# Retention layer and quantised FFN on one core: order of block 0's last products and turns, a weight-rounding clump moved by a step, the last FFN's first products, and the tail's rstd on ScalarE

## The chip, the cores and the metric

The kernel runs on 1 core of one Trainium2 chip. The metric is the device time of one execution in microseconds (us). Times given as "the median" come from 3 runs; everything read from the trace comes from one profiled execution.

## The reference, cut to what matters

The input `x` has 4 sequences of 1024 tokens with 512 features, so 4096 rows. All arithmetic is in float32.

```python
def layernorm(x): return (x - mean(x)) / sqrt(var(x) + 1e-5)          # over the 512 features

def retention(x):
    q, v = x @ Wq.T, x @ Wv.T
    ret = scan(v)              # per sequence: state = lam * state + v_t, one lam for each head
    y = layernorm(q * ret) * gamma + beta
    return (y * silu(x @ Wg.T)) @ Wo.T

def ffn(x):                    # gate_w, up_w, down_w are first rounded to float8 e4m3 values
    gate = silu((x @ gate_w) * gate_scale)
    return ((gate * ((x @ up_w) * up_scale)) @ down_w) * down_scale   # 512 -> 1536 -> 512

x1  = x  + layernorm(retention(layernorm(x)))
out = x1 + layernorm(ffn(layernorm(x1)))
```

## The kernel before, in words

The 4096 rows are cut into 8 blocks of 512 tokens (`NB = 8`, `TB = 512`), each of four subtiles of 128 tokens (`NS = 4`). The 512 features are four chunks of 128 (`NC = 4`), and the FFN's 1536 hidden features are 12 chunks (`NI = 12`). Blocks are software-pipelined. In the main loop over `t` the FFN of block t (`f`, class `Ffn`) runs with the retention part of block t+1 (`b`, class `Retention`), the first steps of block t+2 (`n`) and the last steps of the FFN of block t-1 (`l`). The inner loop over `i` from 0 to 11 takes one hidden chunk in each step: `f.gate(i)` (tile `pfg`), one product of the retention of `b`, `f.up(i)` (tile `pfu`), and `f.down(i - f.lag)` (tiles `pd`; lag 2, in the last block 4).

The order on every engine is the order of the Python code: all instructions are kept in program order by the wrapper `InOrder`. So an instruction that waits holds up all that stand behind it on its engine. Each helper call puts its instructions at that place in the queue of each engine that it uses.

Steps that the change touches:

- `turn_x(s)` turns a subtile of the next block's normalised x on TensorE (tile `ptx`). `keep_x(s)` copies it into `xnT`, on ScalarE for s = 0 and 1 and on VectorE for s = 2 and 3. The pool that holds `xnT` has one buffer for it, so block 1's `xnT` takes the place of block 0's, whose last reader is the product `a.gate(3)` (tile `pg`).
- `var()` is the matmul that averages the squares (`sqsum`, summed on GpSimd) over the features; ScalarE takes the square root and `rstd_y()` is VectorE's reciprocal of 128x512.
- `q(c)` is the product with `wq_sb` (tile `pq`); `y_of(c)` is its VectorE product with the scanned `ret`.
- `turn_x1n(s)` (tile `pt`), `upper_of(s)` (ScalarE) and `rest_of(s)` (VectorE) make the two parts of `x1nT`, which `f.gate` and `f.up` read. Two parts, a rounded one and its remainder, stand in for one float32 operand; all products of the FFN run over both.
- `rounds(3)` rounds one of the 18 weight pieces to float8 values: three VectorE operations on 128x1024 (tile `scr`). `units()` issues the two ScalarE operations of 128x1024 that belong to it; `rounds(3)` calls it straight away unless `now=False`. All but the first eight pieces are loaded by SP's queue when an earlier piece is finished.
- `halves()` splits a sum in two parts (`half`): a copy on ScalarE, then a subtraction on VectorE. In step i = 4 the two parts feed the two matmuls of `var()`.
- In the tail, after the loop, each subtile s goes through `scale`, `stats` (VectorE), `rstd`, `norm` and `add`. `rstd(s)` is `rstd_in_place`: two operations on a 128x1 operand on GpSimd. `norm` runs on ScalarE for s < 3 (`shift_scale`: three operations) and on VectorE for s = 3.

Of the kernel before, what the change touches and what calls it, by code (L numbers as in the profile page):

```python
# [14 lines left out]
AF = mybir.ActivationFunctionType  # L15
# [8 lines left out]
def retention_ffn_sandwich(  # L24
# [23 lines left out]
    NI = I // P  # L48
    TB = 512
    NS = TB // P  # L50
# [15 lines left out]
    class InOrder:  # L66
# [9 lines left out]
    pe, dve, act, pool, sp = (  # L76
        InOrder(e) for e in (nc.tensor, nc.vector, nc.scalar, nc.gpsimd, nc.sync)
    )
# [16 lines left out]
    def load_square(src, name):  # L95
        w = wpool.tile([P, NC, D], F32, tag=name, name=name)
        v = src.rearrange("(c p) f -> p c f", p=P)
        for h in range(2):
            sp.dma_start(w[:, 2 * h : 2 * h + 2, :], v[:, 2 * h : 2 * h + 2, :])
        return w  # L100
# [3 lines left out]
    wq_sb = load_square(wqT, "wq_sb")  # L104
# [29 lines left out]
    eps_sb = const.tile([P, 1], F32, tag="eps_sb", name="eps_sb")  # L134
# [80 lines left out]
    def units():  # L215

        while open_units:
            _, c = open_units.pop(0)
            act.activation(c, c, AF.Relu, bias=neg_low)
            act.activation(c, c, AF.Identity, scale=1.5 * 2.0**20, bias=low_unit)  # L220

    def rounds(n, now=True):
        for _ in range(n):
            next(rounding, None)
            if now:
                units()
# [35 lines left out]
    def rstd_in_place(var, n):  # L262
        pool.tensor_scalar(var, var, EPS, 1.0, ALU.add, ALU.mult)
        pool.tensor_tensor(var, var, nhalf[:, :n], ALU.pow)
# [17 lines left out]
    def project(po, w, col, parts, tokens=slice(None)):  # L282


        out = po.rearrange("p (g j) -> p g j", j=Q) if len(parts[0].shape) == 4 else po
        for c in range(NC):
            for h, part in enumerate(parts):
                pe.matmul(
                    out[:, tokens], w[:, c, ts(col, P)], part[:, c, tokens],
                    start=(c == 0 and h == 0), stop=(c == NC - 1 and h == len(parts) - 1),  # L290
                )
# [3 lines left out]
    def ps_tile(name, home="pa"):  # L295
        return homes[home].tile([P, TB], F32, tag=home, name=name)
# [20 lines left out]
    class Retention:  # L317
# [88 lines left out]
            )  # L406
            dve.tensor_copy(carry[:, c : c + 1], ret[:, TB - 1 : TB])

        def q(self, c, home="pa"):
            self.pq[c] = ps_tile(f"pq_{self.t}_{c}", home)  # L410
            project(self.pq[c], wq_sb, c, [self.by_chunk])

        def y_of(self, c):

# [133 lines left out]
    class Ffn:  # L548
# [68 lines left out]
        def rstd(self, s=None):  # L617
            if s is None:
                rstd_in_place(self.mv[:, :, 1], NS)
            else:  # L620
                rstd_in_place(self.mv[:, s, 1:2], 1)

        def norm(self, s, center=center_scale):
            center(self.d[s], self.d[s], self.mv[:, s, :])

# [46 lines left out]
    early, later = slice(0, TB // Q // 2), slice(TB // Q // 2, TB // Q)  # L672
# [17 lines left out]
    b = Retention(1)  # L690
# [33 lines left out]
        b.norm_x(s, True)  # L724
    rounds(6, now=False)
    a.gate(2, "pf")
    a.var()
    a.rstd_y()
    a.silu(2)
    b.new_xnT()  # L730
    b.turn_x(0, "pd0")
    b.turn_x(1, "pd1")
    a.gate(3, "pf")
    b.turn_x(2, "pd2")
    b.turn_x(3, "pd3")
    b.keep_x(0)
    b.keep_x(1)
    b.keep_x(2, dve.tensor_copy)
# [39 lines left out]
    b.q(0, "pf")  # L778
    a.turn_x1n(1)
    a.upper_of(1)  # L780
    a.turn_x1n(2)
    a.upper_of(2)
    a.x1_moments(3)
    a.x1n_of(3)
    a.rest_of(1)
    b.y_of(0)
    a.rest_of(2)
    b.q(1, "pf")
    rounds(3, now=False)
    a.turn_x1n(3)  # L790
    a.upper_of(3)
    units()
    a.rest_of(3)
    b.y_of(1)
# [4 lines left out]
    l = None  # L799
    for t in range(NB):  # L800
        f, n = Ffn(a), None
        for i in range(NI):
            if t > 0 and (t > 1 or i):
                (f if i else l).rest((i - 1) % NI)
            if t == 0 and i == 0:
                n = Retention(2)
# [32 lines left out]
                next(search)  # L839

            if b and t == 0 and i < 2:
                b.q(i + 2)
                b.y_of(i + 2)
            if b and t > 0 and i < 3:
                b.v(i + 1)
# [15 lines left out]
                    n.shift()  # L861
            if b and i == 4:
                b.halves()
                b.g_of(1)
                b.var()
            if b and i == 5:
# [27 lines left out]
                b.turn_x1n(3, "pf")  # L894
                b.upper_of(3)
            if t == 0:
                if i < 8:
                    rounds(3, now=i == 3)
                f.rest(i)
                if i < 3:  # L900
                    n.stats(i)
# [36 lines left out]
                n.send_x(2 * i - 9)  # L938
            if n and i == (9 if t else 7):
                n.fetch_x()  # L940
            if b and not n and i == 11:
                b.turn_x1n(3)
                b.upper_of(3)
            if b and i == 11:
                b.rest_of(3)
            if n and i == 11:
                n.q(0)
# [3 lines left out]
                f.sums()  # L951
            if f.lag <= i < (NI if b else NI - 1):
                f.down(i - f.lag)
            elif l and i < 2:
                l.down(NI - 2 + i)
            if b and i == 4 and 0 < t < NB - 2:
                n = Retention(t + 2)
            if t == 2 and i == 1:
# [5 lines left out]
        l, a, b = f, b, n  # L964
# [14 lines left out]
    for s in range(NS):  # L979
        l.scale(s)  # L980
        l.stats(s)
        l.rstd(s)
        if s < NS - 1:
            l.norm(s, shift_scale)
        if s == 2:
            l.add(0, dve)
    l.add(1, dve)
    l.add(2, dve)
    l.norm(3)
    l.add(3, dve)  # L990

# [43 lines left out]
```

## Time and profile before

| what | value |
|---|---|
| median of 3 runs | 1011.26 us (1011.08 to 1011.37) |
| the profiled execution's own time | 1010.72 us |
| its span, first to last instruction | 1008.9 us |
| TensorE (PE) busy | 991.4 us, 98% of the span |
| VectorE (DVE) busy | 633.8 us, 63% |
| ScalarE (ACT) busy | 328.0 us, 33% |
| GpSimd (POOL) busy | 241.2 us, 24% |
| mean granted TensorE clock | 0.997 |
| DMA | 73.79 MB, 73 GB/s over the span |

All instructions carry line L74, that of the wrapper, so instructions are told apart by their tiles. A product of four 128x512 float32 matmuls shows in the trace as 8 matmuls, 3.43 us long where TensorE has no gap (`pq`, `pg`, `pv`, `po`). A product of the FFN, 8 matmuls of 128x512 over the two parts, takes 1.81 to 1.83 us (`pfg`, `pfu`, `pd`). A turn of four 128x128 takes 0.44 us. Times of single instructions below are from the span's start.

### The profile page before, as it was taken

Reading aid. Unit: us, or ns where it says so; the run is one execution under the profiler, and the core shown is the slowest. Engines: PE = TensorE matmul, PEld = TensorE weight load, DVE = VectorE, ACT = ScalarE, POOL = GpSimd, SP = SyncE. Lnnn points to the kernel's source line nnn. Section 1 sums busy time; section 2 is a strip of 40 time slices with the busy share of each in tenths; the row PEclk is TensorE's granted clock in tenths of the full one; section 3 lists DMA queues with packets and bytes.
Section 4 is the critical chain, followed back from the end, with each engine's and each line's share of the span. In section 5 each row is a group of like instructions: output and inputs, shape, how many; then the busy total and the mean of one; then the engine's idle time right before and its main releaser. Section 6 shows DMA issues by size and latency. Waiting matters only on the chain.

```text
span 1008.9 us, 9809 instructions
## 1 busy us (share of the span) xinstructions
PE 991.4 (98%) x3502; PEld 652.7 (65%) x3502; DVE 633.8 (63%) x945; ACT 328.0 (33%) x489; POOL 241.2 (24%) x290
## 2 busy tenths in 40 slices
PE   9999989999999999999999999999999999999997
PEld 7454756666666666666666666666666756766885
DVE  5996878436767286663767547674576735746444
ACT  3546555524765124111321113211141111412222
POOL 1405131202322042221403114131142302213021
PEclk9999999999999999999999999999999999999999
DMA  9312213400126004250113402043020520004021
GB/s 302 106 62 97 97 58 89 141 1 21 63 74 157 0 22 146 84 146 1 39 56 104 115 1 84 11 128 92 0 84 32 136 63 7 37 22 125 1 84 42
DMA packets 62608, 73.79 MB, mean 73 GB/s; under 512 B 5856, under 2 KB 36320, under 8 KB 62560
## 3 DMA queue, kind: packets, MB, share of 16 engines
q1 hardware_dynamic: 60976, 72.24, 23.6%
q10 hardware_dynamic: 1584, 0.94, 0.4%
q8 instruction: 27, 0.44, 0.2%
q14 instruction: 21, 0.17, 0.1%
HBM read 43.53 MB, written 29.62 MB: 73 GB/s over the span
## 4 chain that ended last, share of the span: by engine, by line
PE 91%; DVE 3%; POOL 2%; ACT 2%; DMA 1%; issue 0%; ACTq 0%; SPq 0%; POOLq 0%; DVEq 0%
PE pfu L74 17%; PE pfg L74 16%; PE pd L74 16%; PE pv L74 11%; PE pq L74 10%; PE pg L74 10%; PE po L74 10%; DVE scr L74 1%; POOL sqsum L74 1%; DMA xnT<-mx 1%; POOL x L74 1%; POOL mv L74 0%; DVE st L74 0%; PE var L74 0%; ACT scr L74 0%
## 5 line engine op out<-in xcount | busy, mean ns | idle before, releaser
L74 PE MATMUL pfu<-x1nT,up_sb 128*128 128x512 f32 x768 | 217.1, 425 | 0.0
L74 PE MATMUL pfg<-x1nT,gate_sb 128*128 128x512 f32 x768 | 190.2, 390 | 1.1 <-ACT x1nT L74 0.7
L74 PE MATMUL pd<-down_sb,fuse 128*128 128x512 f32 x720 | 188.4, 403 | 0.0
L74 PEld LDWEIGHTS pfu<-x1nT,up_sb 128*128 128x128 f32 x768 | 145.4, 189 | 56.0 <-issue 29.2
L74 PEld LDWEIGHTS pfg<-x1nT,gate_sb 128*128 128x128 f32 x768 | 143.9, 188 | 31.7 <-DVE x1nT L74 1.0
L74 PEld LDWEIGHTS pd<-down_sb,fuse 128*128 128x128 f32 x720 | 135.4, 188 | 38.2 <-issue 10.8
L74 ACT CAST fuse<-gate 128x512 fp32r<-128x512 f32 x90 | 55.7, 619 | 275.0 <-DVE gate L74 275.0
L74 ACT ACTIVATE gate<-pfg,gs_sb 128x512 f32<-128x512 f32 x96 | 65.9, 687 | 225.1 <-PE pfg L74 225.0
L74 DVE SCALAR_TENSOR_TENSOR gate<-pfu,us_sb,gate 128x512 f32<-128x512 f32 x96 | 71.7, 747 | 105.9 <-PE pfu L74 105.7
L74 PE MATMUL pv<-xnT,wv_sb 128*128 128x512 f32 (+1 forms) x280 | 114.9, 556 | 1.3 <-ACT xnT L74 1.1
L74 PE MATMUL pq<-xnT,wq_sb 128*128 128x512 f32 x256 | 114.9, 592 | 0.0
L74 PE MATMUL pg<-xnT,wg_sb 128*128 128x512 f32 x256 | 114.8, 592 | 0.0
L74 PE MATMUL po<-wo_sb,y 128*128 128x512 f32 x256 | 114.5, 592 | 0.0
L74 POOL TENSOR_SCALAR mv<-mv 128x1 f32<-128x1 f32 (+1 forms) x77 | 19.0, 247 | 315.4 <-DVE mv L74 314.7
L74 PEld LDWEIGHTS pv<-xnT,wv_sb 128*128 128x128 f32 x280 | 52.7, 189 | 48.6 <-issue 44.0
L74 DVE TENSOR_TENSOR fuse<-gate,fuse 128x512 fp32r<-128x512 f32 x90 | 79.4, 883 | 6.9 <-ACT fuse L74 6.9
L74 PEld LDWEIGHTS po<-wo_sb,y 128*128 128x128 f32 x256 | 48.4, 189 | 50.1 <-issue 47.4
L74 PEld LDWEIGHTS pg<-xnT,wg_sb 128*128 128x128 f32 x256 | 48.4, 189 | 49.6 <-issue 47.0
L74 PEld LDWEIGHTS pq<-xnT,wq_sb 128*128 128x128 f32 x256 | 47.9, 189 | 49.0 <-issue 47.4
L74 POOL TENSOR_TENSOR x<-x,x1n 128x512 f32<-128x512 f32 x32 | 49.2, 1536 | 44.3 <-DVE x1n L74 35.4
L74 DVE TENSOR_TENSOR_SCAN ret<-lam,pv 128x512 f32<-128x512 f32 x16 | 19.5, 1220 | 54.5 <-PE pv L74 54.5
L74 DVE BATCH_NORM_STATS2 st<-x 128x6 f32<-128x512 f32 x64 | 43.5, 680 | 13.6 <-POOL x L74 11.3
(112 smaller groups left out, 923.0 us busy)
## 6 DMA issues: line engine op xcount, KB each, us to landing
kept<-x SPq DMA_DIRECT2D x32, 256.0 KB, 2.1
x<-kept SPq DMA_DIRECT2D x32, 256.0 KB, 3.9
x<-in_x SPq DMA_DIRECT2D x28, 256.0 KB, 3.8
out<-d SPq DMA_DIRECT2D x27, 256.0 KB, 2.0
xnT<-mx SPq DMA_DIRECT2D x24, 256.0 KB, 4.7
mxs<-xs SPq DMA_DIRECT2D x84, 64.0 KB, 1.8
x1n<-mxs SPq DMA_DIRECT2D x21, 256.0 KB, 2.6
mx<-xn SPq DMA_DIRECT2D x20, 256.0 KB, 2.1
```

What stands on the lines that cost most here:

```text
L74: return lambda *args, **kwargs: tc.keep_in_program_order(op(*args, **kwargs))
```

## The change

There are five edits.

1. In block 0, the four `turn_x` of block 1 stand ahead of `a.var()`; before, two stood behind it and two behind `a.gate(3)`.
2. `b.q(1)` is cut into two halves of 256 tokens, set between the turns of `x1n`; the first half of `b.q(2)` moves from the main loop to the place behind the last turn, in the memory of `pd0`.
3. In the main loop of t = 0, the rounding of one piece moves from the end of step 3, with its ScalarE part at once, to step 4 behind `b.halves()`, with its ScalarE part issued later in that step by `units()`.
4. In t = 6, the last step's turn of `x1n` moves behind `f.down(9)`, and `f.down(10)` follows it there; it stood in the first step of t = 7, and `l.down(11)` moves from the second step of t = 7 to the first.
5. In the tail, `rstd(s)` becomes a square root on ScalarE and a 128x1 reciprocal on VectorE, and the additions of s = 0, 1 and 2 all stand behind the loop.

```diff
-        def q(self, c, home="pa"):
-            self.pq[c] = ps_tile(f"pq_{self.t}_{c}", home)
-            project(self.pq[c], wq_sb, c, [self.by_chunk])
+        def q(self, c, home="pa", tokens=slice(None)):
+            if c not in self.pq:
+                self.pq[c] = ps_tile(f"pq_{self.t}_{c}", home)
+            project(self.pq[c], wq_sb, c, [self.by_chunk], tokens)
...
+        def rstd_by_root(self, s):
+            var = self.mv[:, s, 1:2]
+            act.activation(var, var, AF.Sqrt, bias=eps_sb)
+            dve.reciprocal(var, var)
...
     a.gate(2, "pf")
+    b.new_xnT()
+    for s in range(NS):
+        b.turn_x(s, f"pd{s}")
     a.var()
     a.rstd_y()
     a.silu(2)
-    b.new_xnT()
-    b.turn_x(0, "pd0")
-    b.turn_x(1, "pd1")
     a.gate(3, "pf")
-    b.turn_x(2, "pd2")
-    b.turn_x(3, "pd3")
     b.keep_x(0)
...
     a.turn_x1n(1)
     a.upper_of(1)
+    b.q(1, "pf", early)
     a.turn_x1n(2)
     a.upper_of(2)
+    b.q(1, "pf", later)
     a.x1_moments(3)
     a.x1n_of(3)
     a.rest_of(1)
     b.y_of(0)
     a.rest_of(2)
-    b.q(1, "pf")
     rounds(3, now=False)
     a.turn_x1n(3)
     a.upper_of(3)
+    b.q(2, "pd0", early)
     units()
     a.rest_of(3)
     b.y_of(1)
...
             if b and t == 0 and i < 2:
-                b.q(i + 2)
+                b.q(i + 2, tokens=slice(None) if i else later)
                 b.y_of(i + 2)
...
             if b and i == 4:
                 b.halves()
+                if t == 0:
+                    rounds(3, now=False)
                 b.g_of(1)
                 b.var()
...
             if t == 0:
-                if i < 8:
-                    rounds(3, now=i == 3)
+                if i < 8 and i != 3:
+                    rounds(3, now=False)
                 f.rest(i)
...
-            if b and not n and i == 11:
-                b.turn_x1n(3)
-                b.upper_of(3)
-            if b and i == 11:
+            if b and n and i == 11:
                 b.rest_of(3)
...
             if f.lag <= i < (NI if b else NI - 1):
                 f.down(i - f.lag)
-            elif l and i < 2:
-                l.down(NI - 2 + i)
+            elif l and i < 2 and (b or i == 0):
+                l.down(NI - 2 + i if b else NI - 1)
+            if b and not n and i == 11:
+                b.turn_x1n(3)
+                b.upper_of(3)
+                b.rest_of(3)
+                f.down(NI - 2)
...
     for s in range(NS):
         l.scale(s)
         l.stats(s)
-        l.rstd(s)
+        l.rstd_by_root(s)
         if s < NS - 1:
             l.norm(s, shift_scale)
-        if s == 2:
-            l.add(0, dve)
-    l.add(1, dve)
-    l.add(2, dve)
+    for s in range(NS - 1):
+        l.add(s, dve)
     l.norm(3)
     l.add(3, dve)
```

## The prediction

> **What bounds the kernel now.** The page first: TensorE is busy nearly throughout, so a gain lies in its gaps or in the tail behind its last matmul.
>
> ```profile
> PE 991.4 (98%) x3502; PEld 652.7 (65%) x3502; DVE 633.8 (63%) x945; ACT 328.0 (33%) x489; POOL 241.2 (24%) x290
> ```
>
> Then TensorE's waits (total us, times, longest). Apart from the start and waits of 0.3 or less there are six, and the edits stand at all of them: block 0's `var` (0.9), the turns (`pt`) and first FFN product after block 0 (1.0, 0.7, 0.5), `var` of step 4 (3.6), the last turn at 930 us (0.8).
>
> ```profile
> PE var L74 <- ACT half L74: 3.6, 1, 3.6
> ...
> PE pt L74 <- ACT x1n L74: 1.0, 1, 1.0
> PE var L74 <- POOL sqsum L74: 0.9, 1, 0.9
> PE pt L74 <- DVE x1n L74: 0.8, 1, 0.8
> PE pfg L74 <- ACT x1nT L74: 0.7, 1, 0.7
> PE pfg L74 <- DVE x1nT L74: 0.5, 1, 0.5
> ```
>
> Third, the timeline (start, us, instruction) at the longest: ScalarE, then TensorE. `half` sits behind two `scr`, and the `pfu` after the gap takes 3.57 us where 1.98 is usual (1.81 without the overlap of neighbours). The windows table says why: clock 0.50.
>
> ```profile
> 130.87 1.14 ACT L74 ACTIVATE scr<-scr,neg_low 128x1024 f32<-128x1024 f32 x1
> 132.05 1.15 ACT L74 ACTIVATE scr<-scr,low_unit 128x1024 f32<-128x1024 f32 x1
> 133.10 0.67 ACT L74 ACTIVATE gate<-pfg,gs_sb 128x512 f32<-128x512 f32 x1
> 133.67 0.60 ACT L74 CAST half<-sqsum 128x512 fp32r<-128x512 f32 x1
> ...
> 134.33 0.50 PE L74 MATMUL var<-half,mean_r 128*128 128x512 f32 x1 [3.58 <-ACT half L74]
> ...
> 135.39 3.57 PE L74 MATMUL pfu<-x1nT,up_sb 128*128 128x512 f32 x8
> ...
> 136.00:138.00 2.00, 2.00 (x7) 0.50 0.01 3
> ```
>
> Last, the tail's timeline: GpSimd's `mvd` holds back VectorE's last `d`, but two additions run beside it.
>
> ```profile
> 1003.04 0.18 DVE L74 BATCH_NORM_AGGREGATE mvd<-st 128x2 f32<-128x6 f32 x1
> 1003.14 1.27 DVE L74 TENSOR_TENSOR d<-d,x 128x512 f32<-128x512 f32 x2
> ...
> 1003.94 0.88 POOL L74 TENSOR_TENSOR mvd<-mvd,nhalf 128x1 f32<-128x1 f32 x1
> 1004.85 0.55 DVE L74 TENSOR_SCALAR d<-d,mvd 128x512 f32<-128x512 f32 x1 [0.44 <-POOL mvd L74]
> 1005.43 0.76 DVE L74 TENSOR_TENSOR d<-d,x 128x256 f32<-128x256 f32 x2
> ```
>
> **What the Trainium skill says.** "TensorE: Matmul & The Clock Gate", Part 1: TensorE falls to half clock after an idle window of about 3.4 us. The trace agrees: 3.58 us idle, then half clock. "ScalarE: Activation LUTs", What ACT_TABLE_LOAD costs: a load is about 1.28 us (here 1.28, at 134.79) and an ACTIVATE 186 ns plus 0.833 an element, 93 ns more for each pointer operand (128x1 here: 0.20 and 0.29). Same page, Table sets: cheap functions are in every set, so the tail needs one load; the trace agrees, the `scr` at 130.87 ran without one. "SBUF — State Buffer", Who interferes with whom: VectorE and GpSimd lock each other out of a shared port; a `scr` addition beside GpSimd's `ysum` took 2.13 us at 97.43, against 1.22.
>
> **Part by part.** Times are those of before; shifts are added.
>
> Turns before `var`: `pg` ends at 49.43 and `var` waits for GpSimd's `sqsum` until 50.36. Now four turns (4 x 0.44, their last input ready at 49.86) fill that to 51.17; `var` takes 0.87, the last `pg` 3.43, so it ends at 55.47. ScalarE's copies into `xnT` wait for this `pg`, the last reader of the one buffer; two copies take 1.08 with the hops 1.15, so `pv` starts at 56.62, against 56.96. Two turns that used to run beside the copies no longer do, so TensorE idles 1.15 there where it idled 0.29: this edit moves a wait more than it removes one. The square root ends 0.55 later, at 52.8, but VectorE takes the reciprocal only at 53.77, behind a `scr`; that cover is 1 us. VectorE's copies of s = 2, 3 end at 58.25, just as the second half of `pv` comes up (56.62 + 1.72 = 58.34). **-0.34**, passed on whole by the chain `po`, moments, `x1`, in which VectorE idles 0.63 before the first `po`'s statistics.
>
> `q` in halves: between the second turn (88.42) and the seven `pfg` matmuls (96.19), TensorE does three turns, one `pq` and one `pfg` matmul, 3 x 0.44 + 3.43 + 0.23 = 4.98 us of work in 7.77. The end of the stretch is set by VectorE's last `x1nT`, behind a clump (92.46 to 95.5). VectorE's queue there is not changed, so 96.19 stays, but half of `pq` 2 (3.43/2 = 1.72) is by then done and missing later. Cover: the third turn moves from 90.0 to 90.6 behind half a `pq`, and ScalarE's `x1nT` with it to 91.8, still in time for VectorE at 91.86; the fourth turn starts when its input is ready, near 93.1, against 93.94. Were that cover gone, each tenth late is a tenth lost. **-1.72**. VectorE can follow: it has gaps of 0.7, 1.2 and 1.2 before 110.5.
>
> The clump: no GpSimd operation is moved. SP's load of a later piece, issued by the clump, moves with it by some 3 us; its reader stands two clumps on, over 10 us later. Without the two `scr` (130.87 to 133.10) ScalarE reaches `half` 2.23 earlier, at 131.44; its input `sqsum` is ready at 130.6, so the wait cannot shrink by more than 0.8 beyond this. VectorE's part of `half` follows directly at 132.07, since the clump now stands behind it. TensorE's gap shrinks from 3.58 to 1.35: **-2.23**. No whole window is idle then, and gaps of 0.9 to 1.0 left full clock, so `pfu` should take 1.83 instead of 3.39: **-1.56**. The price: VectorE's `half` ends at 132.76, and the clump (0.6 + 1.22 + 1.22) puts its `gate` of step 4 at 135.8, 3.2 earlier where TensorE gains 3.8. Behind it stand the reciprocal (3.34), the next clump and z(0), whose end frees the buffer of ScalarE's next `gate` (147.92 to 148.6), which frees the memory that `pfg` takes at 149.55. That is 0.95 of slack, less 0.6: free, but any further lateness above 0.35 becomes a new TensorE wait.
>
> Last block: from `pfu` of step 11 to the first `pfg` of the next FFN it took 5.13 us (927.22 to 932.35). Now pfu 1.81, pd 1.81 and turn 0.44 are 4.06; the second pd, 1.81, only moves here from the next step. The turn's input is ready at 929.95, while pd(9) runs until 930.84; ScalarE's and VectorE's parts of `x1nT` then end at 932.8, under pd(10), before 933.1. The queues of VectorE, ScalarE, SP and GpSimd keep their order. **-1.07**.
>
> Tail: the table load fits ScalarE's idle stretch (993.94 to 997.36). Each s now stops VectorE, with the next `scale` queued behind: hop 0.08, root 0.29, hop 0.03, reciprocal 0.17. Root and reciprocal of 128x1 have no row: the root from the 128x1 with a pointer (0.2 to 0.4), the reciprocal from VectorE's 128x1 copy, 0.15 (to 0.3; I exclude faster than a copy). Run through, `scale` of s = 1, 2, 3 starts at 997.83, 999.96, 1002.09 (before 997.25, 999.32, 1001.58), and the last reciprocal ends at 1004.29. Only then come three additions of 0.64, which had run in GpSimd's or TensorE's shadow, `norm` 0.55 and the halves 0.76: 1007.4 against 1006.19. The GpSimd pairs that go had cost this path only the 0.44 that VectorE waited before the last `norm`. The three stores come closer to the last; 256 KB at the 380 GB/s seen there is 0.7, against an addition every 0.64, so they queue by 0.2 at most. **+1.2** (0.7 to 1.8).
>
> Sum: -0.34 - 1.72 - 2.23 - 1.56 - 1.07 + 1.2 = -5.7. On the profiled execution (1010.72, span 1008.9 and 1.8 around it) that gives 1005.0; the median stands 0.54 higher: **1005.5**.
>
> **Rivals.** *VectorE keeps what TensorE gains:* from 110.5 to 124.3 it works without a gap; if port locks against GpSimd's sums eat its 3.1 us of gaps before, the first two gains (0.34 + 1.72 = 2.1) end there: 1007.6. Against: the one lock seen cost 0.9.
> *The clock stays low:* 1.35 idle plus neighbours could still count as an idle window: +1.56, 1007.1. Against: about 1.1 idle at 95 to 96 was followed by full clock.
> *Both*, with the dear tail (+0.6): 1009.3, within 0.2%.
> *A dear reciprocal:* the only shape in the trace is 128x512, 3.34 us. If 128x1 cost that whatever the size, four would stand one after the other on VectorE in the tail: 4 x (3.34 - 0.17) = 12.7 more, 1018.2. It decides from (5.7 + 2)/4 + 0.17 = 2.1 us each. Against: 3.34/512 is 6.5 ns an element, and VectorE's other 128x1 take 0.15 to 0.18. That the gaps do not set the end at all is excluded by the chain of waits, 91% of it TensorE.
>
> **How the numbers follow.** A measurement can tell about 0.2% (2 us) from no change. Forecast 0.64, VectorE 0.12, clock 0.12, both 0.08, reciprocal 0.04. The first three are faster: 0.88; 0.08; 0.04. The range starts at 1003.8 (tail at +0.7, a lock less, the run's spread) and ends at 1008.2 (either single rival with 0.6 of a dear tail).
>
> **What would show it.** Right: no `pt` wait of 0.8 or more, `var` of step 4 waiting near 1.4, its `pfu` near 1.9, the last addition some 1.2 later behind the last `pd` than now. Wrong: `pfu` above 3; new waits of `pfg` or `po` on VectorE between 110 and 170; a 128x1 reciprocal over 1 us; a second table load in the tail.

## The result, and the profile after

| | before | after |
|---|---|---|
| median of the runs compared | 1011.17 us (1009.91 to 1012.15, 6 runs) | 1006.38 us (1005.76 to 1008.49, 6 runs) |
| the profiled execution: time, span | 1010.72, 1008.9 us | 1006.49, 1004.7 us |
| TensorE busy | 991.4 us | 988.9 us |

The kernel is faster by 4.8 us: the ratio is 0.9957, with a 95% interval of 0.9945 to 0.997, which is 3.0 to 5.6 us. The predicted 1005.5 is 0.9 below the median. The interval lies below no change, the profiled spans differ by 4.2 us, and the sum of the prediction was 5.7. The question is where the missing part went.

The page's line of busy times, after:

```profile
PE 988.9 (98%) x3518; PEld 653.6 (65%) x3518; DVE 633.8 (63%) x949; ACT 330.1 (33%) x494; POOL 234.8 (23%) x282
```

TensorE's busy time fell by 2.5 us, 1.8 of it on the group `pfu` (217.1 to 215.3 on the pages). The rest of the gain is idle time that went, less the idle time that the start and the tail have added. The list of TensorE's waits shows it (total us, times, longest):

```profile
PE pv L74 <- ACT xnT L74: 2.7, 2, 1.5
PE var L74 <- ACT half L74: 1.4, 1, 1.4
PE pv L74 <- DMA xnT<-mx: 1.3, 2, 0.7
```

Set this beside the list of before. Gone are the waits of `var` on GpSimd (0.9), of `pt` on VectorE (0.8), of `pfg` on ScalarE (0.7), and 0.7 of the other `pt` wait (1.0, now 0.3). `var` waits 1.4 where it waited 3.6. Two lines have grown: `pv` on ScalarE's `xnT` from 1.1 to 2.7 (of it 1.17 for block 1, which edit 1 makes; the rest is the start of the kernel), and `pv` on the DMA `xnT<-mx`, which the prediction does not have, to 1.3. In the list of before that line was the last but one, and small:

```profile
PE pv L74 <- DMA xnT<-mx: 0.2, 1, 0.2
```

The timeline (start, us, instruction, idle before) at the longest wait, after, and the windows table there (stretch, length, then TensorE's busy time, its clock as the first number without a count, the DMA share):

```profile
129.28 0.68 ACT L74 ACTIVATE gate<-pfg,gs_sb 128x512 f32<-128x512 f32 x1
129.86 0.61 ACT L74 CAST half<-sqsum 128x512 fp32r<-128x512 f32 x1
130.52 0.50 PE L74 MATMUL var<-half,mean_r 128*128 128x512 f32 x1 [1.38 <-ACT half L74]
131.57 1.99 PE L74 MATMUL pfu<-x1nT,up_sb 128*128 128x512 f32 x8
...
132.00:134.00 2.00, 2.00 (x10) 1.65 (x9) 1.97 (x2) 1.99 (x3) 0.00 (x0) 1.00 0.00 0
```

Only one pair of `scr` (126.55 to 128.86) now stands ahead of `gate` and `half` where there were two, the wait is 1.38 instead of 3.58, and `pfu` behind it took 1.99 instead of 3.57: in this execution the clock stayed at 1.00.

The tail's timeline, after, last subtile:

```profile
998.43 0.29 ACT L74 ACTIVATE mvd<-mvd,eps_sb 128x1 f32<-128x1 f32 x1 [0.33 <-DVE mvd L74]
998.76 0.16 DVE L74 RECIPROCAL mvd<-mvd 128x1 f32<-128x1 f32 x1 [0.36 <-ACT mvd L74]
998.84 1.87 DVE L74 TENSOR_TENSOR d<-d,x 128x512 f32<-128x512 f32 x3
...
1001.21 0.76 DVE L74 TENSOR_TENSOR d<-d,x 128x256 f32<-128x256 f32 x2
```

Root and reciprocal are as short as forecast. But VectorE waits 0.36 for the root with nothing to do, and then does the three additions while its `norm`, which starts at 1000.63, is ready to run.

Now the accounts of the two profiled executions, each number a difference of two start or end times on the timelines:

| place | predicted | measured |
|---|---|---|
| first `pv` (start of the kernel) | - | +0.40 |
| block 1's `pv` (edit 1), start taken off | -0.34 | -0.33 |
| `pfu` of step 1 (edit 2) | -1.72 | -1.67 |
| wait of `var` in step 4 (edit 3) | -2.23 | -2.2 |
| `pfu` behind it (edit 3) | -1.56 | -1.57 |
| last FFN's first products (edit 4) | -1.07 | -1.03 |
| tail, from the last `pd` to the end (edit 5) | +1.2 | +1.03 |
| between 144 and 921 us | 0 | +1.24 |

They sum to -4.1 against the span's -4.2. The start differs in every profile: the first `pv` stands between 9.21 and 10.02 us in the kernels below, before's at 9.62, with no order by edit; it is not counted to the change.

### The profile page after: what moved, and what is told of

It reads as the page before. It is cut to its first block, busy times and chain, and to the rows that moved or that the text cites. A ratio compares the mean times of both kernels' runs of the same rounds, so it can differ in the third digit from the quotient of the medians.

```text
span 1004.7 us, 9838 instructions
## 1 busy us (share of the span) xinstructions
PE 988.9 (98%) x3518; PEld 653.6 (65%) x3518; DVE 633.8 (63%) x949; ACT 330.1 (33%) x494; POOL 234.8 (23%) x282
## 4 chain that ended last, share of the span: by engine, by line
PE 90%; DVE 4%; DMA 2%; ACT 1%; POOL 1%; issue 1%; SPq 0%; DVEq 0%; POOLq 0%
PE pfu L74 16%; PE pfg L74 16%; PE pd L74 16%; PE pv L74 11%; PE pg L74 10%; PE pq L74 10%; PE po L74 9%; DMA xnT<-mx 1%; DVE scr L74 1%; DMA mx<-xn 1%; DVE st L74 1%; POOL x L74 1%; DVE d L74 1%; DVE xn L74 0%; DMA beta_sb<-in_beta 0%
## 5 line engine op out<-in xcount | busy, mean ns | idle before, releaser
L74 PE MATMUL pfu<-x1nT,up_sb 128*128 128x512 f32 x768 | 215.3, 422 | 0.0
L74 PE MATMUL pq<-xnT,wq_sb 128*128 128x512 f32 (+1 forms) x272 | 115.3, 567 | 0.0
L74 PEld LDWEIGHTS pq<-xnT,wq_sb 128*128 128x128 f32 x272 | 50.8, 190 | 46.8 <-issue 44.5
```

Source lines behind the costliest of these rows:

```text
L74: return lambda *args, **kwargs: tc.keep_in_program_order(op(*args, **kwargs))
```

## The experiments

Each kernel was timed beside the kernel before on the same chip, another chip in each of the three comparisons; that kernel's median was 1011.47, 1011.32 and 1011.54 us there. Ratios are to it, and kernels of different comparisons are best set side by side by their ratios. An interval is about 0.1% wide on either side, 1 us, so small terms are read from the traces.

### The first comparison: edits 1, 2 and 3 alone, and the gap filled

**Edit 1 alone.** The four `turn_x` ahead of `a.var()`:

```diff
+    b.new_xnT()
+    for s in range(NS):
+        b.turn_x(s, f"pd{s}")
     a.var()
```

> The kernel before with only the turns ahead of var. Theory: var no longer waits for sqsum (0.9), but pv waits 1.15 for ScalarE's copies instead of 0.29; pv starts 0.3 earlier relative to the pg before it; 0.3 us less, not to be told from none in the times. Rival (the turns pay in full): 0.9 less.

Measured: 1011.44 us (13 runs), ratio 0.9998, interval 0.9989 to 1.0006. In its trace `var` has no wait and `pv` waits 1.16. The moved wait is as expected; a gain of a third of a microsecond can't be told by the times.

**Edit 2 alone.** `q` in halves:

```diff
+    b.q(1, "pf", early)
     a.turn_x1n(2)
     a.upper_of(2)
+    b.q(1, "pf", later)
...
+    b.q(2, "pd0", early)
```

> The kernel before with only q 1 in halves and half of q 2 moved. Theory: the seven pfg matmuls still start 96.2 us in or so, set by VectorE's last x1nT; pfu of step 1 ends 1.7 earlier (108.7 against 110.4) and VectorE follows; the wait of var in step 4 stays 3.6; 1.7 us less, 1009.5. Rival (VectorE keeps it): pfu of step 1 ends earlier, but the stretch up to var of step 4 ends where it did, near 134.3, and the time stays.

Measured: 1010.9 us (13 runs), ratio 0.9998, interval 0.999 to 1.0006. In the trace TensorE's gain arrives: `var` of step 4, which hangs on VectorE's and ScalarE's work, stands 1.68 earlier than before when the start is taken off. So VectorE does follow. But the times show at most 1 us of it, and the list of TensorE's waits, in which `var` still has its 3.6, has more of the line of which before had 0.2:

```profile
PE pv L74 <- DMA xnT<-mx: 1.0, 2, 0.6
```

The two are at 440.89 (0.61) and 806.92 (0.43). This is the part that the prediction lacks. The list does not tie it to edit 2 yet: on this line edit 1 alone has 0.6, edit 3 alone and the kernel with the gap filled have 0.7 each, and edits 4 and 5 alone have nothing. What sets edit 2 apart comes in the third comparison.

**Edit 3 alone.** The clump in step 4 behind `b.halves()`:

```diff
                 b.halves()
+                if t == 0:
+                    rounds(3, now=False)
                 b.g_of(1)
...
-                if i < 8:
-                    rounds(3, now=i == 3)
+                if i < 8 and i != 3:
+                    rounds(3, now=False)
```

> The kernel before with the moved clump alone. Theory (half stood behind two scr on ScalarE, and the 3.58 us gap cost half clock): var of step 4 waits 1.4 us instead of 3.6, the pfu behind it takes 1.83 instead of 3.39, no half clock in the trace before the end; 3.8 us less, 1007.4 if before is at 1011.2. Rival (the clump only pays with the earlier turns and products): the wait stays above 2.5 or a new wait of pfg or po on VectorE's z follows between 140 and 170 us; less than 2 us gained.

Measured: 1008.7 us (1007.02 to 1009.45, 8 runs), ratio 0.9972, interval 0.9961 to 0.9982: a gain of 2.8 us, between the wait alone (2.23) and wait and clock (3.79). Its profiled execution was the slowest of the eight; timeline and windows:

```profile
132.39 0.50 PE L74 MATMUL var<-half,mean_r 128*128 128x512 f32 x1 [1.36 <-ACT half L74]
133.45 3.21 PE L74 MATMUL pfu<-x1nT,up_sb 128*128 128x512 f32 x8
...
134.00:136.00 2.00, 2.00 (x6) 1.55 (x5) 1.97 (x2) 1.96 (x4) 0.00 (x0) 0.50 0.00 0
```

The wait is the same 1.36, and yet the clock fell to 0.50 and `pfu` took 3.21. So a gap of this size leaves full clock in some executions and not in others.

**The gap filled.** The kernel before, with three needless matmuls in the gap, so that the wait of `var` is the same but TensorE is not idle:

```diff
             var = ps_tile(f"var_{self.t}")
+            if self.t == 1:
+                for _ in range(3):
+                    pe.matmul(var, mean_w, wq_sb[:, 0, :], start=True, stop=True)
```

> The kernel before with three needless products of 128x512 (0.86 us each) into var's tile ahead of its two matmuls in step 4; nothing else changes, so var still starts when half is ready, near 134.3. Theory (idleness brings the half clock): the pfu behind var takes 1.83 instead of 3.39 us and the time falls by 1.6, to 1009.6. Rival (pfu is slow for another reason, such as the transfers that run at 134 to 136 us, or the clock falls anyway): pfu stays near 3.4 and the time stays at 1011.2 or rises.

Measured: 1010.16 us (21 runs), ratio 0.9987, interval 0.9981 to 0.9994: 1.3 us faster (0.6 to 1.9), by doing more work. The timeline:

```profile
134.33 0.50 PE L74 MATMUL var<-half,mean_r 128*128 128x512 f32 x1 [1.03 <-ACT half L74]
...
135.40 2.01 PE L74 MATMUL pfu<-x1nT,up_sb 128*128 128x512 f32 x8
```

The three matmuls run from 130.57 to 133.31, `var` starts at 134.33 as in the kernel before, and `pfu` takes 2.01 instead of 3.57. So the half clock is caused by the idle time: the trace has 1.56 for it, as predicted, and the times agree with that.

### The second comparison: edits 4 and 5 alone, and two sums

**Edit 4 alone.** The last turn and `f.down(10)` at the end of the last step of t = 6:

```diff
+            if b and not n and i == 11:
+                b.turn_x1n(3)
+                b.upper_of(3)
+                b.rest_of(3)
+                f.down(NI - 2)
```

> The kernel before with only the last FFN's first products reordered. Theory: no wait of pt at 930 us; from pfu of step 11 to the first pfg of the last FFN 5.9 us with two pd instead of 5.1 with one, so 1.0 less; 1010.2. Rival (the gap moves to pfg, which waits for x1nT): no difference.

Measured: 1010.09 us (21 runs), ratio 0.999, interval 0.9983 to 0.9996: 1.0 us faster (0.4 to 1.7). The wait of `pt` near 930 is gone. The step holds, on the times too.

**Edit 5 alone.** Root and reciprocal in the tail, and the additions behind them:

```diff
-        l.rstd(s)
+        l.rstd_by_root(s)
...
-        if s == 2:
-            l.add(0, dve)
-    l.add(1, dve)
-    l.add(2, dve)
+    for s in range(NS - 1):
+        l.add(s, dve)
```

> The kernel before with the new tail alone. Theory: everything up to the last pd as before; from the last pd's end to the last addition's end 5.7 instead of 4.7; 1.0 more, 1012.2. Rival (the tail's cost seen in the changed kernel came from earlier work of VectorE): no difference.

Measured: 1012.0 us (13 runs), ratio 1.0007, interval 0.9999 to 1.0015: slower by 0.7 at the middle, which fits the price of 1.0 but does not exclude none. The trace has it without doubt: from the last `scale` to the last addition's start 4.44 us, and 3.85 before; the last `scale` itself stands 0.43 later behind the last `pd`.

**Edits 1 to 4 with the old tail.** The changed kernel, less edit 5:

```diff
-        l.rstd_by_root(s)
+        l.rstd(s)
...
-    for s in range(NS - 1):
-        l.add(s, dve)
+        if s == 2:
+            l.add(0, dve)
+    l.add(1, dve)
+    l.add(2, dve)
```

> The changed kernel with the tail of before (rstd on GpSimd, additions where they stood). Theory (the new tail costs 1.0 to 1.2): from the last pd's end to the last addition's end it takes 4.7 us as before, instead of 5.7; 1.0 less than the changed kernel, 1005.2. Rival (the new tail saves GpSimd's 0.44 wait and the rest is hidden): 1006.4 or more.

Measured: 1006.22 us (1004.65 to 1007.08, 5 runs), ratio 0.9945, interval 0.9932 to 0.9957. The same as the whole change within what these runs can tell. Its trace has the tail as short as expected, 4.70 us from the last `pd`'s end to the last addition's end (5.73 with edit 5), but its profiled execution had the half clock: `var` waited 1.37, and `pfu` took 3.42.

**Edits 1 to 4, and the root for the last subtile only**, beside the two additions that VectorE has to do anyway. Against the kernel just above; the first root, of a constant, makes ScalarE load its table ahead of the tail:

```diff
+    act.activation(low_unit, eps_sb, AF.Sqrt)
...
-        l.rstd(s)
         if s < NS - 1:
+            l.rstd(s)
             l.norm(s, shift_scale)
...
+    var = l.mv[:, 3, 1:2]
+    act.activation(var, var, AF.Sqrt, bias=eps_sb)
     l.add(1, dve)
     l.add(2, dve)
+    dve.reciprocal(var, var)
     l.norm(3)
```

> As the changed kernel, but in the tail only the last subtile takes its rstd by the square root, with two additions between the root and the reciprocal; s = 0 to 2 and the additions stand as before, and a root of a constant loads the table while ScalarE is idle. Theory (what costs in the new tail is VectorE's stop in each subtile and the additions behind the last reciprocal): from the last aggregate's end the last norm starts 1.3 us later instead of 1.63 before; 0.3 less than with the old tail, 1004.9. Rival (the root itself is dear): not below the old tail.

Measured: 1005.24 us (1004.5 to 1005.91, 5 runs), ratio 0.9939, interval 0.9925 to 0.9952. Its tail:

```profile
997.26 1.27 DVE L74 TENSOR_TENSOR d<-d,x 128x512 f32<-128x512 f32 x2
997.43 0.28 ACT L74 ACTIVATE mvd<-mvd,eps_sb 128x1 f32<-128x1 f32 x1
998.45 0.16 DVE L74 RECIPROCAL mvd<-mvd 128x1 f32<-128x1 f32 x1
```

The root runs under the additions and VectorE does not wait for it. From the start of the last `pd` group (994.54) to that of the last addition (999.23) it is 4.69 us; before it is 5.01, after 6.04. So in the last subtile the root and the fast reciprocal are worth 0.32; as edit 5 places them, in every subtile and with all additions behind, the tail is 1.35 longer than that.

### The third comparison: the two remaining waits

What stood open was the 1.24 us between 144 and 921 us, and the clock. The distances from one middle block's turns (`pt`) to the next's are the same in all kernels within some hundredths (121.78 us), but for two blocks, those with the `pv` that waits on the DMA (122.04 and 122.25 before, 122.94 and 122.64 after). The rows of SP's queue at the first of these, before and then after, with the `pv` that waits:

```profile
431.64 0.32 SPq L74 DMA_DIRECT2D mx<-xn  x1
433.73 1.92 SPq L74 DMA_DIRECT2D xnT<-mx  x4
```

```profile
426.19 0.32 SPq L74 DMA_DIRECT2D mx<-xn  x1
429.37 1.91 SPq L74 DMA_DIRECT2D xnT<-mx  x4
436.80 3.67 PE L74 MATMUL pv<-xnT,wv_sb 128*128 128x512 f32 x8 [0.66 <-DMA xnT<-mx]
```

`xnT` is fetched from what `mx` has written, so SP waits for the last `mx` to land: 2.09 us from issue to issue before, 3.18 after. At this place `pv` did not wait before and waits 0.66 after; a fetch that is issued 1.1 later costs 0.66, so it had some 0.4 us to spare.

What makes the write late stands in the list of DMA queues (queue, kind: packets, MB, share of the 16 engines) and of transfers (the last number: us to landing), in the 3.6 us from 0.49 ahead of the issue of `mx`. Before, 431.15 to 434.75:

```profile
q1 hardware_dynamic: 297, 0.53, 39.2%
...
mx<-xn SPq DMA_DIRECT2D x1, 256.0 KB, 2.0
```

After, 425.70 to 429.30:

```profile
q1 hardware_dynamic: 288, 0.52, 39.2%
q8 instruction: 1, 0.02, 2.4%
...
mx<-xn SPq DMA_DIRECT2D x1, 256.0 KB, 3.1
```

After, one packet of 16 KB of the queue of kind "instruction" lies at the write, from 425.81 to 427.21. Nearly all packets of the write have ended by 427.82; the last dozen end one after the other, 0.08 us apart, until 428.88. That looks as if they stood behind the large packet on one DMA engine, though the trace does not name the engine of a packet. The traces of all 14 kernels hold 70 such writes ahead of a fetch in the middle blocks. At 10 of them an instruction packet is under way in the time between the issue of the write and that of the fetch; these 10 take 2.7 to 3.6 us from issue to issue, the other 60 take 2.04 to 2.13. The 10 are the two places in each of the five kernels that have edit 2 and fetch where the kernel before does.

The smaller waits fit too. Where an instruction packet lies beside the fetch instead of the write (before: from 803.84 to 805.26, ahead of the wait of 0.23 at 807.16), `pv` waits 0 to 0.64; where none lies at either, it does not wait. The packets come in every kernel, 27 of them, one for about 260 of TensorE's matmuls and weight loads (7061 / 27), so they are probably TensorE's own program. Edit 2 adds 16 matmuls and 16 weight loads (the x3502 and x3518 of the pages), and in these five kernels two of the packets fall on the two writes, where in the kernels without it they come later. No run moved the packets alone.

**Edit 2 undone in the version with the root for the last subtile only**, on which all kernels of this comparison stand:

```diff
-    b.q(1, "pf", early)
...
-    b.q(1, "pf", later)
...
+    b.q(1, "pf")
...
-    b.q(2, "pd0", early)
```

> The change without its q in halves (edit 2), with the old tail and a square root on ScalarE for the last subtile only. Theory: q in halves brings 1.7 us at the first FFN and some 1.0 of it is lost again at the two late fetches of xnT near 440 and 807 us, so its net is about 0.6: this kernel takes 0.4 to 0.9 us more than the same with edit 2 (1005.24 in the last comparison), in its trace the time from the issue of the last mx to that of xnT is 2.1 us at both places, and the waits of pv on xnT's fetch are 0.2. Rival: the late fetches have nothing to do with edit 2; then they are seen here too, and this kernel is 1.7 slower. Second rival: with the other edits made, edit 2 brings nothing.

Measured: 1005.64 us (1004.47 to 1007.42, 5 runs), ratio 0.9943, interval 0.9931 to 0.9956. From `mx` to `xnT` it is 2.10 and 2.06 at the two places, and TensorE's list has no wait on this DMA. The time is 0.4 above that with edit 2: as the theory has it, though the second rival, that edit 2 brings nothing, is not excluded by runs that spread over 3 us. The rival that the late fetches have nothing to do with edit 2 falls. Its profile shows the half clock too: `pfu` took 3.44 behind a wait of 1.37.

**x sent and fetched a step earlier.**

```diff
-            if n and t > 0 and 6 <= i <= 9:
-                n.norm_x(i - 6)
-                n.send_x(i - 6)
+            if n and t > 0 and 6 <= i <= 8:
+                for s in (2, 3) if i == 8 else (i - 6,):
+                    n.norm_x(s)
+                    n.send_x(s)
...
-            if n and i == (9 if t else 7):
+            if n and i == (8 if t else 7):
                 n.fetch_x()
```

> Edits 1 to 4 with the root for the last subtile, and x of the next block's third and fourth subtile both sent in step 8 and fetched there, a step earlier than before. Theory: pv's two waits on xnT's fetch (1.2 us together in the trace without this) vanish, and since the fetch then has over 3 us to spare, the time falls by 0.8 to 1.2. Rival: two more operations of VectorE in step 8 hold up gate and the x1nT parts behind them, and TensorE waits there in each of six blocks instead: same or slower.

Measured: 1003.35 us (1002.77 to 1005.0, 5 runs), ratio 0.9925, interval 0.9911 to 0.9938. TensorE's list of waits, the second to fourth line:

```profile
PE var L74 <- ACT half L74: 1.4, 1, 1.4
PE idle L74 <- DVE nhalf L74: 1.0, 1, 1.0
PE pfg L74 <- DVE x1nT L74: 0.4, 1, 0.4
```

The DMA's line is gone and nothing new has come: the rival, VectorE held up in step 8, falls. Against the same kernel with the later fetch, the two distances between turns fall from 123.22 and 122.31 to 122.04 and 121.78, 1.7 us in all, of which 1.2 are the listed waits. The spans differ by 1.2 (1002.7 and 1001.5), since this kernel happened to start 0.4 later; the medians differ by 1.9, the ratios by 1.4 us: somewhat more than the 0.8 to 1.2 expected. Here the last `mx` was issued at 420.20 and `xnT` at 422.28, 2.08 later, although edit 2 is in: the instruction packet comes at 429.13, when the write is long done.

**One needless matmul in the gap ahead of `var`**, as above with one instead of three.

> Edits 1 to 4 with the root for the last subtile, and one needless 128x512 matmul of float32 (0.87 us) in the gap that is left ahead of var in step 4. Theory: the half clock that follows this gap of 1.4 us in some executions comes from its idle time; with 0.5 us idle it never comes, every run has a mean clock of 0.998 or more before the end, and the median falls by 0.2 to 0.5 (a fifth to a half of the runs lost 1.6 us to it). Rival: the half clock comes from elsewhere; then some runs still show it and the median stays.

Measured: 1004.26 us (1003.64 to 1004.63, 5 runs), ratio 0.9928, interval 0.9916 to 0.9941. `var` waits 0.52, `pfu` takes 2.02, and the granted clock of all five runs is 0.998 or 0.999 (0.997 to 0.999 without the matmul, so this says little). The median is 1.0 below that without it, more than the 0.2 to 0.5 expected; in the two profiled executions 0.5 of this is in the waits on the DMA, 0.7 here and 1.2 there, which this edit was not made for.

**Both.**

> The last two together: earlier sending and fetching of x, and one needless matmul in the gap ahead of var of step 4. If both theories hold the gains add up: 1.0 to 1.6 us below the kernel without either (1005.24 in the last comparison). If only one holds, it equals that one.

Measured: 1003.11 us (1002.79 to 1003.65, 4 runs), ratio 0.9918, interval 0.9904 to 0.9931: the fastest, 8.3 us below the kernel before (7.0 to 9.7). Its interval lies wholly below that of the change itself (0.9945 to 0.997). Against 1005.24 it is 2.1 us, more than the 1.0 to 1.6 expected; the two gains alone were 1.9 and 1.0. With a few runs of each, a microsecond of that is within the spread.

## Why the prediction was right or wrong

- **The direction and the size** were right: 1006.38 lies in the range (1003.8 to 1008.2).
- **Turns before `var`**: right, -0.33 for -0.34. It moves a wait (1.17 at `pv`) more than it removes one.
- **`q` in halves**: right where it was read, -1.67 for -1.72, and the cover held: the fourth turn did start when its input was ready, at 93.27, after a wait of 0.28. **The step that failed** is what lies behind it: the prediction followed the gain through VectorE and ScalarE to 170 us and then took it as passed on to the end. Part of it is given back at two late fetches: `pv` waits 1.28 there, 0.23 before, since an instruction packet now falls on each of the two writes that they wait for, which land 1.1 and 1.3 us later, and the fetches had only about half a microsecond to spare. Over the kernels this `pv` waits 0 to 0.7 without edit 2 and 0.7 to 1.3 with it where the fetch stands as before (means of the traces: 0.33 and 1.10). The line of 0.2 in the list of before was set aside as small ("apart from the start and waits of 0.3 or less"), while it was a sign that this DMA chain had little to spare.
- **VectorE keeps what TensorE gains** (rival): falls. There are no new waits on VectorE between 110 and 170 us, although a `scr` at 102.48 took 0.99 instead of 0.68.
- **The clump, wait**: right to a few hundredths. The slack named for the later `gate` held: `pfg` at 144.10 has no wait.
- **The clump, clock**: right in the profiled execution, wrong as a sure thing. The forecast was that no whole window is idle and that full clock stays. Of six profiled executions with the gap of 1.4 us, the half clock followed in three (edit 3 alone, edits 1 to 4, edit 2 undone), and not in the other three. With the gap of 3.6 it followed in all five profiled (before and edits 1, 2, 4 and 5 alone), with the gap filled in none of three. So the rival "the clock stays low" holds in part of the runs, which moves the mean as an estimate by 0.8 if it is half of them (half of 1.56).
- **The Trainium skill**, "TensorE: Matmul & The Clock Gate", Part 1, gives an idle window of about 3.4 us for the fall to half clock. The gap of 1.4 us with 0.2 between the two `var` behind it fell short of this and still brought half clock in half of the profiles; the measurement decides.
- **What may decide it in those 1.6 us**: the clock records of the traces say more. Between their first and their last change all stretches are whole multiples of 3.413 us (before: 129.706, 3.413 and 866.985 us are 38, 1 and 254 of them), so the clock is set in steps. Summed over each step, TensorE's recorded idle time ahead of a fall to half clock in the main loop is 1.58 to 2.90 us, never a whole step, not even with the gap of 3.58 that the prediction took for agreement. The gap of 1.4 lies whole in one step in four kernels (1.58 or 1.60 idle): edit 3 alone, edits 1 to 4 and edit 2 undone got half clock, x fetched a step earlier did not. It is cut by the end of a step in two (1.07 and 0.54 in the changed kernel, 0.26 and 1.35 with the root for the last subtile), and both kept full clock. In all 14 traces no step at full clock with 1.54 idle or less was followed by half clock, and 22 of the 23 with 1.58 or more were (8 in the main loop, 14 at the ends of the kernels). No run shifted the gap against the steps on purpose, so that this decides it is likely and not shown.
- **Last block**: right, -1.03 for -1.07.
- **A slip in the sum of the rival "Both"**: 1005.5 + 2.1 + 1.56 + 0.6 is 1009.8 and not 1009.3; it was not the case that came.
- **Tail**: right in sign and cause, +1.03 for +1.2. Root (0.29) and reciprocal (0.16) were priced right, so the rival of a dear reciprocal falls. "ScalarE: Activation LUTs", What ACT_TABLE_LOAD costs, has 1.28 us for a table load; it took 1.28 at 988.70, hidden in ScalarE's idle stretch, and there was no second one in the tail.

What stays open: how the added instructions move the packets to just these places, which no run tried alone; and why one of the four gaps of 1.4 us that lie whole in a step left full clock.

## What to carry to other kernels

A wait of 0.2 us on a transfer says that its chain has little to spare: before counting on a gain upstream, look what each later transfer still has to spare, down to the end of the kernel and not only over the next stage. When a transfer lands late without a reason in the program, look at the queues that the program does not fill: the instruction packets move with the number of instructions, and an edit that adds some can put one onto a critical transfer. Shortening a gap is worth more than its length when the clock falls behind it, and filling it with needless work is enough to show that; but a gap cut to less than half of a step of the clock (1.4 us here) is not a safe one. In a tail, an operation on a faster engine helps only if the waiting engine has something to do meanwhile: the additions put beside the root gave 0.3, the same operations ahead of all additions cost 1.0.

## What the runs showed of the hardware that was not expected

A TensorE gap of 1.36 to 1.38 us brought a stretch at half clock in three of six profiled executions and none in the others (`pfu` 3.21 to 3.44 us, or 1.99 to 2.02); the clock changed only at steps of 3.413 us, and fell only after steps in which TensorE was idle for 1.58 us or more. And a 256 KB write to DRAM took 2.04 to 2.13 us from its issue to the issue of its reader at 60 places, but 2.7 to 3.6 us at the 10 at which a 16 KB packet of the instruction queue was under way at the same time.
